# Two graph-attention layers in one kernel: the adjacency cast to bf16 in DRAM and turned by a transposing DMA, layer 0's TensorE work in smaller pieces

## The chip, the cores and the metric

The kernel runs on one core of a Trainium2 chip. The metric is the device time of one launch in microseconds (us). The kernel before took 3321.95 us, the median of three runs (3321.3 to 3324.14).

## What is computed

Sixteen graphs of 1024 nodes with 256 features each pass through two attention layers. Both use the same adjacency, which holds 0 or 1. Cut to what matters:

```python
# layer 0, per graph; 4 heads of 64
h = x @ W                                         # per head
weight[i, j] = leaky_relu(e_src[i] + e_dst[j]) where adj[i, j], else -1e9
o = relu(softmax(weight) @ h + bias) + h
x = layernorm(x + layernorm_per_head(o) * ln_gamma + ln_beta)
# layer 1, per graph; 8 heads of 32
n = layernorm(x) * gamma1 + beta1
attn = softmax(where(adj > 0, n @ n.T / sqrt(32), -inf)) @ n
x = x + attn
x = layernorm(x + gelu(layernorm2(x) @ W1 + b1) @ W2 + b2)
```

The adjacency arrives as 32-bit integers with queries as rows. The kernel wants it as a mask of one byte with keys on the partitions, so every 1024 x 1024 adjacency has to be cast and turned.

## The kernel before

**Two streams.** `layer0()` (line 987) and `layer1()` (line 1005) are Python generators. Each runs over the sixteen graphs, and layer 0 works on graph b+1 while layer 1 works on graph b. The order of instructions on TensorE, VectorE, ScalarE and GpSimd is the order in which Python issues them: the loop at lines 1058 to 1076 takes one step of one stream or of the other. A stream yields after each step with a number (how far it has come) and with the things that its next step needs. `COURSE` (line 1043) says how far layer 0 is to be for each point of layer 1, and `SLACK` how far it may stray from that when the stream that is due would have to wait. Small chains of VectorE, ScalarE and GpSimd work (normalisations, residuals) wait in a list, and `advance()` (line 466) issues those whose inputs are due. Only SyncE's queue, which carries DMAs, is ordered by the framework.

**Layer 0.** `prepare` (line 504) takes two blocks of 128 rows at a time. It turns x on TensorE (`transpose_rows`), multiplies with `w0e` (W and two extra columns per head; tile `ph`, 264 wide, two chunks of 128 in the contracted dimension, line 546), and evicts. `turn_mask` (line 509) takes one block `ak` of 128 adjacency rows, turns its eight 128 x 128 pieces on TensorE as bf16 into one PSUM bank, and writes them as the mask with one `Square` on ScalarE, which also counts the neighbours. The block comes by a casting DMA on GpSimd's queue (`load_adj`, line 492); three blocks are in flight (`load_adj(i + 3)`, line 523). `attention0` (line 587) has 32 steps per graph. A step's weights are two VectorE operations of 128 x 512 (line 598), issued three steps ahead (`AHEAD`), and its products are 16 matmuls in 64-column tiles (line 612).

**Layer 1.** `attention1` (line 740) has 32 steps per graph. A step computes four logit tiles (line 766, four matmuls with 32 rows each, side by side in the array), four exponentials on ScalarE (line 772), two VectorE products with the mask (line 778), and, three steps later, the products with the values (line 780). `mlp` (line 893) follows, in units of 16 matmul records.

**PSUM.** Four banks `ps` take logits and the first half of the MLP; two `po` take layer 1's sums; two `acc` (through `bank0`, line 390) take all of layer 0's: x turned, mask turned, `ph`, products, and a few transposes of layer 1 during its attention. A matmul with fp32 operands is two records in the trace, a bf16 transpose one.

Of the kernel before, what the change touches and what calls it, by code (L numbers as in the profile page):

```python
# [32 lines left out]
BF16 = mybir.dt.bfloat16  # L33
# [6 lines left out]
P = 128  # L40
# [143 lines left out]
def fast_path(  # L184
# [24 lines left out]
    nc = Pace(tc.nc)  # L209
    B, N, D = x.shape  # L210
    H0, _, HO = w0.shape
# [29 lines left out]
    memory = ctx.enter_context(tc.tile_pool(name="memory", bufs=2, space=bass.MemoryType.DRAM))  # L241
# [247 lines left out]
    adj_blocks = {}  # L489
    x_blocks = {}  # L490

    def load_adj(i):
        b, k = divmod(i, NB)
        if b < B:
            ak = adj_blocks[i] = three.tile([P, N], BF16, name="ak")
            nc.gpsimd.dma_start(ak, adj[b, k * P : (k + 1) * P, :])

    def load_blocks(i):
        b, k = divmod(i, NB // GB)
# [4 lines left out]
    def prepare(b, hb, esr, cbs, v0, dinv, mask):  # L504

        def turn_mask(k):
            i = b * NB + k  # L510
            ak = adj_blocks.pop(i)
            pt, _ = bank0([P, NB, P], BF16)
            for j in range(NB):
                nc.tensor.transpose(pt[:, j, :], ak[:, j * P : (j + 1) * P], identb)
            nc.scalar.activation(
                mask[k // BPH][:, :, k % BPH * P : (k % BPH + 1) * P],
                pt,
                AF.Square,
                bias=shift_c,
                scale=-(NEAR0 + NEAR1),  # L520
                accum_out=types[:, i : i + 1],
            )
            load_adj(i + 3)

        turning, scaling = [], []
        for k in range(0, NB, GB):
            i = b * (NB // GB) + k // GB
            load_blocks(i + 1)
            xk = x_blocks.pop(i)
            xT = one.tile([P, DC, GB * P], F32, name="xT")  # L530
            transpose_rows(xT, xk)
            yield 0.45, bank0_ready
            turn_mask(k)
            yield 0.5, bank0_ready, xT
            if k % BPH == 0:

                finish_norms(b - 1, k // BPH)
                hb.append(one.tile([P, BPH, D], F32, name=f"hb{k // BPH}"))
            for g in range(GB):
                if g == 0:  # L540

                    for chain in turning:
                        complete(chain)
                ph, _ = bank0([P, D + 2 * H0])
                for c in range(DC):
                    nc.tensor.matmul(ph, xT[:, c, g * P : (g + 1) * P], w0e[:, c, :], start=c == 0, stop=c == DC - 1)
                nc.scalar.copy(apart[g][:, :, 0], ph[:, D + H0 : D + 2 * H0])
                nc.scalar.activation(v0[:, k + g, :, HO], ph[:, D : D + H0], AF.Exp)
                nc.scalar.activation(dinv[:, k + g, :], ph[:, D : D + H0], AF.Exp, scale=-0.99)
                scaling.append(values0(v0[:, k + g, :, :], ph))  # L550
                begin(scaling[-1], "vector", ph)
                nc.scalar.copy(hb[-1][:, (k + g) % BPH, :], ph[:, 0:D])
                yield 0.9, bank0_ready
                if g == 0:
                    turn_mask(k + 1)
                    yield 0.5, bank0_ready, xT
# [30 lines left out]
    def attention0(b, hb, v0, esr, cbs, dinv, factors, mask, rinv):  # L587

        groups = [(n, pair) for n in range(NH) for pair in range(H0 // PAIR)]
        steps = [(n, hd, j) for n in range(NH) for hd in range(H0) for j in range(0, NB, PAIR)]

        def weights(n, hd, j):
            cb = cbs[n, hd // PAIR]
            p = four.tile([P, PAIR, HALF], F32, name="p0")
            for i in range(PAIR):
                nc.vector.scalar_tensor_tensor(
                    p[:, i, :],
                    cb[:, hd % PAIR, :],  # L600
                    dinv[:, j + i, hd : hd + 1],
                    mask[n][:, j + i, :],
                    op0=OP.max,
                    op1=OP.mult,
                )
            return p

        def products(p, hd, j, av):
            for i in range(PAIR):
                for q in range(BPH):  # L610
                    for at in range(0, P, TILE):
                        nc.tensor.matmul(
                            av[at : at + TILE, q, :],
                            p[:, i, q * P + at : q * P + at + TILE],
                            v0[:, j + i, hd, :],
                            start=j + i == 0 and q == 0,
                            stop=j + i == NB - 1 and q == BPH - 1,
                        )

        nc.vector.tensor_copy(factors, v0[:, :, :, HO])  # L620

        ps = [weights(*step) for step in steps[:AHEAD]]
        yield 1.0, bank0_ready, ps[0]
        for i, (n, hd, j) in enumerate(steps):
            if j == 0:
                av, bank = bank0([P, BPH, HO + 1])
                bank["busy"] = True
            products(ps.pop(0), hd, j, av)
            advance()
            if i + AHEAD < len(steps):  # L630
                ps.append(weights(*steps[i + AHEAD]))
            if j == NB - PAIR * AHEAD and hd % PAIR == PAIR - 1 and (n, hd // PAIR) in groups[:-2]:

                at = groups[groups.index((n, hd // PAIR)) + 2]
                cbs[at] = spread_factor(esr, *at)
            if j == NB - PAIR:
                h = hb[n][:, :, hd * HO : (hd + 1) * HO]
                residual = residual0(av, h, rinv[:, n * BPH : (n + 1) * BPH, hd])
                residuals[b, n, hd] = residual
                bank["busy"] = False  # L640
                bank["readers"] = [residual]
                begin(residual, "vector", av)
                if hd % PAIR == PAIR - 1:
                    norms[b, n, hd] = after0(b, n, hd, hb[n])
                    begin(norms[b, n, hd], "vector", done(residual), hb[n])
            yield (1.0, *ps[:1], *([bank0_ready] if j == NB - PAIR else []))

    def residual0(av, h, rinv):

# [384 lines left out]

    WORK0 = NB // GB * 3.25 + 2.0 + NB * H0 * 1.0
    REST1 = 3.5 * GB
    ATTN1 = REST1 + 2.0 + 2.5 * (NH * NB * H1 // QUAD)
    WORK1 = ATTN1 + NB // GB * (1.75 * FC / 2 + 3.5 * GB) - REST1  # L1040
    SLACK = 0.083
    STAY = 0.017
    COURSE = [(0.0, 1.0), (REST1, 1.0), (ATTN1, 1.32), (WORK1 - 12.0, 2.0), (WORK1, 2.0)]

    def wanted():
        b, done = place[1]
# [477 lines left out]
```

## Time and profile before

| | us |
|---|---|
| median of three runs | 3321.95 |
| the profiled execution, own time | 3326.4 |
| its span, first to last instruction | 3324.5 |
| TensorE busy (weight loads apart) | 3227.9 |
| VectorE busy | 2887.0 |
| ScalarE busy | 1944.0 |
| GpSimd busy | 546.5 |

In the trace one graph's layer 1 begins about every 201 to 207 us; the graph used below begins at 717.9 us and the next one at 919.3. From 717.9 to 843.0 lies its attention (with what is left of the MLP of the graph before at the front), from 843.0 to 919.3 its MLP. Layer 0's `prepare` for the next graph goes from 719.6 to 799.4. The first 110 us hold layer 0 of graph 0 alone, and after 3145 layer 1 of the last graph runs alone.

How to read it: busy time of TensorE is that of pipelined matmuls whose ends are modelled, so "busy" can hide a wait. More is learnt from the starts of consecutive groups in the timeline: from the start of one group to the start of the next is what it cost the engine. All helper-recorded operations stand under line 61; they are told apart by their tiles, such as `acc<-identb,ak` for the mask turned, `acc<-w0e,xT` for the product with W, `acc<-v,p` for layer 0's products, `ps<-nT` for layer 1's logits, `po<-p,v`, `po<-p,unit` and `po<-v,p` for layer 1's products, `ps<-yT,w_sb` and `po<-w_sb,hid` for the MLP.

### The profile page before, as it was taken

How to read it: one execution, taken by the hardware profiler on the slowest of the kernel's cores; microseconds unless marked ns; L12 is line 12 of the kernel's file. 1: busy time of each engine (PE TensorE's matmuls, PEld its weight loads, DVE VectorE, ACT ScalarE, POOL GpSimd, SP SyncE). 2: the span in 40 equal slices, each digit the busy share in tenths (PEclk: the TensorE clock that was granted, in tenths of full speed). 3: DMA queues.
4: the chain of work that ended last, by engine and by line, in shares of the span. 5: the costliest groups of instructions: out<-in, count | busy, mean ns of one | idle time of the engine just before them, and what ended most of it. 6: DMA issues, size and time to landing. Idle time of an engine off the chain costs nothing.

```text
span 3324.5 us, 148763 instructions
## 1 busy us (share of the span) xinstructions
PE 3227.9 (97%) x68257; PEld 2050.2 (62%) x68257; DVE 2887.0 (87%) x4943; ACT 1944.0 (58%) x4192; POOL 546.5 (16%) x552
## 2 busy tenths in 40 slices
PE   6899999999999999999999999999999999999988
PEld 4557575665756657566575755757566575665745
DVE  6898897988979889898988979889798898989983
ACT  2564747557375673846647366473755738466473
POOL 1202011020211202112020111202102021120300
PEclk9899999999999999999999999999999999999999
DMA  5201102021120211202112020110202112020000
GB/s 140 53 22 46 42 25 66 14 52 35 31 61 18 52 30 34 60 20 62 23 44 44 25 60 19 50 38 28 63 19 47 35 34 60 19 59 10 24 6 15
DMA packets 94732, 131.79 MB, mean 40 GB/s; under 512 B 9360, under 2 KB 60560, under 8 KB 94096
## 3 DMA queue, kind: packets, MB, share of 16 engines
q1 hardware_dynamic: 74080, 87.58, 8.4%
q0 software_dynamic: 18432, 33.56, 6.6%
q8 instruction: 536, 8.78, 1.1%
q10 hardware_dynamic: 1584, 1.05, 0.1%
q14 instruction: 100, 0.82, 0.1%
HBM read 138.68 MB, written 17.04 MB: 47 GB/s over the span
## 4 chain that ended last, share of the span: by engine, by line
PE 86%; DVE 10%; issue 2%; ACT 1%; DMA 0%; POOL 0%; ACTq 0%; SPq 0%; POOLq 0%; DVEq 0%
PE po L61 34%; PE ps L61 30%; PE acc L61 22%; DVE p L61 8%; DVE o L61 0%; ACT p L61 0%; DVE hb L61 0%; DVE st L61 0%; DVE z L61 0%; ACT oT L61 0%; DMA w0e<-in_L_gnn_W_dram 0%; ACT mask L61 0%; POOL r L61 0%; DVE x L61 0%; DMA v<-in_L_gnn_a_src_dram 0%
## 5 line engine op out<-in xcount | busy, mean ns | idle before, releaser
L61 ACT ACTIVATE p<-ps 128x512 f32<-128x512 f32 x2006 | 1041.0, 611 | 314.7 <-PE ps L61 304.6
L61 DVE TENSOR_TENSOR p<-p,mask 128x1024 f32<-128x1024 f32 x1024 | 1188.7, 1217 | 15.6 <-ACT p L61 15.6
L61 DVE SCALAR_TENSOR_TENSOR p<-cb,dinv,mask 128x512 f32<-128x512 f32 x1024 | 709.5, 743 | 4.1 <-PE acc L61 4.1
L61 PE MATMUL ps<-nT 32*128 32x512 f32 x4012 | 671.9, 643 | 0.0
L61 ACT ACTIVATE hid<-ps,b_sb 128x256 f32<-128x256 f32 x512 | 240.7, 473 | 677.3 <-PE ps L61 677.3
L61 PEld LDWEIGHTS po<-v,p 128*32 128x32 f32 x32768 | 391.5, 109 | 331.0 <-issue 284.6
L61 PE MATMUL acc<-v,p 128*64 128x65 f32 x16384 | 551.8, 225 | 15.8 <-DVE p L61 13.6
L61 PEld LDWEIGHTS acc<-v,p 128*64 128x64 f32 x16384 | 531.4, 139 | 56.9 <-DVE p L61 13.4
L61 PE MATMUL po<-p,v 128*32 128x512 f32 x2048 | 544.3, 606 | 0.0
L61 PE MATMUL po<-p,unit 128*32 128x512 f32 x2048 | 543.6, 606 | 0.0
L61 PE MATMUL po<-w_sb,hid 128*64 128x256 f32 x4096 | 479.5, 381 | 0.0
L61 PE MATMUL ps<-yT,w_sb 128*64 128x256 f32 x4096 | 470.6, 380 | 0.0
L61 PE MATMUL po<-v,p 128*32 128x33 f32 x32768 | 387.8, 198 | 15.7 <-issue 12.0
L61 PEld LDWEIGHTS ps<-yT,w_sb 128*64 128x64 f32 x4096 | 286.3, 137 | 139.7 <-issue 5.3
L61 PEld LDWEIGHTS po<-w_sb,hid 128*64 128x64 f32 x4096 | 279.9, 137 | 133.1 <-issue 3.9
L61 POOL TENSOR_SCALAR r<-mv 128x4 f32<-128x4 f32 (+1 forms) x128 | 87.9, 687 | 1289.2 <-DVE mv L61 1249.1
L61 POOL TENSOR_TENSOR r<-r,mhalf 128x8 f32<-128x8 f32 (+2 forms) x192 | 288.9, 1505 | 16.0
L61 PEld LDWEIGHTS ps<-nT 32*128 32x128 f32 x4012 | 218.0, 184 | 108.1 <-issue 45.0
L61 PEld LDWEIGHTS po<-p,v 128*32 128x32 f32 x2048 | 78.1, 108 | 324.8 <-issue 172.9
L61 DVE TENSOR_TENSOR z<-acc,bias_r 128x256 f32<-128x256 f32 x128 | 54.2, 423 | 209.4 <-ACT hb L61 209.1
L61 POOL DMA_DIRECT2D ak<-in_adj_dram x128 | 71.5, 559 | 961.5 <-PE acc L61 948.9
L61 PE MATMUL acc<-w0e,xT 128*128 128x264 f32 x512 | 151.0, 418 | 9.8 <-issue 6.5
(111 smaller groups left out, 2660.2 us busy)
## 6 DMA issues: line engine op xcount, KB each, us to landing
ak<-in_adj_dram POOLq DMA_DIRECT2D x128, 256.0 KB, 3.9
cb<-esr SPq DMA_DIRECT2D x64, 512.0 KB
xk<-in_x_dram SPq DMA_DIRECT2D x64, 256.0 KB
xl<-in_x_dram SPq DMA_DIRECT2D x32, 512.0 KB
out_dram<-zz SPq DMA_DIRECT2D x64, 256.0 KB
w_sb<-in_L_gnn_W_dram SPq DMA_DIRECT2D x2, 1024.0 KB
esr<-rows SPq DMA_DIRECT2D x64, 4.0 KB
v<-in_L_gnn_a_src_dram SPq DMA_DIRECT2D x2, 320.0 KB
```

The lines of the kernel that those rows point to most:

```text
L61: return method(*args, **kwargs)
```

## The change

For graphs 1 to 15 the adjacency no longer passes through TensorE. `cast_adj(b + 1)`, at the start of `prepare(b)`, issues two DMAs on GpSimd's queue that cast the two halves (512 rows each) of the next graph's adjacency from DRAM to bf16 in DRAM. `load_adj` then fills a block `ak` with two transposing DMAs on SyncE's queue, each 512 rows x 128 columns, and `turn_mask` is the `Square` alone, reading `ak` in SBUF. Graph 0 keeps the old way.

The product with W is cut in two: after the first of the two contracted chunks the stream yields, and `turn_mask` is called there. Its PSUM bank is held over the yield. Layer 0's products are cut in two likewise, one of the two key blocks each, with `advance()` between. The first three weights of a graph are issued with a yield after each. The course is set anew.

```diff
+    def cast_adj(b):
+        if b < B:
+            for n in range(NH):
+                casts[b, n] = memory.tile([HALF, N], BF16, name=f"adjb{n}")
+                nc.gpsimd.dma_start(casts[b, n], adj[b, n * HALF : (n + 1) * HALF, :])
...
             ak = adj_blocks[i] = three.tile([P, N], BF16, name="ak")
-            nc.gpsimd.dma_start(ak, adj[b, k * P : (k + 1) * P, :])
+            if b == 0:
+                nc.gpsimd.dma_start(ak, adj[b, k * P : (k + 1) * P, :])
+                return
+            n, first = divmod(k * PAIR, NB)
+            for e in range(PAIR):
+                nc.sync.dma_start(
+                    ak[:, e * HALF : (e + 1) * HALF],
+                    casts[b, n][:, (first + e) * P : (first + e + 1) * P],
+                    transpose=True,
+                )
...
         def turn_mask(k):
             i = b * NB + k
-            ak = adj_blocks.pop(i)
-            pt, _ = bank0([P, NB, P], BF16)
-            for j in range(NB):
-                nc.tensor.transpose(pt[:, j, :], ak[:, j * P : (j + 1) * P], identb)
+            pt = adj_blocks.pop(i)
+            if b == 0:
...
+            else:
+                n, first = divmod(k * PAIR, NB)
+                dst = mask[n][:, first : first + PAIR, :]
+                pt = pt.rearrange("p (e q) -> p e q", q=HALF)
...
+        cast_adj(b + 1)
...
-            yield 0.45, bank0_ready
-            turn_mask(k)
-            yield 0.5, bank0_ready, xT
+            yield 0.45, bank0_ready, xT
+            if b == 0:
+                turn_mask(k)
+                yield 0.0, bank0_ready, xT
...
-                ph, _ = bank0([P, D + 2 * H0])
+                ph, bank = bank0([P, D + 2 * H0])
+                bank["busy"] = True
                 for c in range(DC):
                     nc.tensor.matmul(ph, xT[:, c, g * P : (g + 1) * P], w0e[:, c, :], start=c == 0, stop=c == DC - 1)
+                    if c == 0:
+                        if b:
+                            turn_mask(k + g)
+                        yield (0.45,)
+                bank["busy"] = False
...
-        ps = [weights(*step) for step in steps[:AHEAD]]
-        yield 1.0, bank0_ready, ps[0]
+        ps = []
+        for step in steps[:AHEAD]:
+            ps.append(weights(*step))
+            yield 0.33, bank0_ready, ps[0]
...
-            products(ps.pop(0), hd, j, av)
+            p = ps.pop(0)
+            products(p, 0, hd, j, av)
+            advance()
+            yield (0.5,)
+            products(p, 1, hd, j, av)
             advance()
...
-            yield (1.0, *ps[:1], *([bank0_ready] if j == NB - PAIR else []))
+            yield (0.5, *ps[:1], *([bank0_ready] if j == NB - PAIR else []))
...
-    WORK0 = NB // GB * 3.25 + 2.0 + NB * H0 * 1.0
+    WORK0 = NB // GB * 2.25 + 2.0 + NB * H0 * 1.0
...
+    SLACK1 = 0.02
-    COURSE = [(0.0, 1.0), (REST1, 1.0), (ATTN1, 1.32), (WORK1 - 12.0, 2.0), (WORK1, 2.0)]
+    COURSE = [(0.0, 1.0), (REST1 + 3.0, 1.0), (ATTN1, 1.31), (WORK1 - 12.0, 2.0), (WORK1, 2.0)]
...
-            allowed = at0 < min(target + SLACK, place[1][0] + 2.05) if other == 0 else at0 > target - SLACK
+            slack = SLACK if place[1][1] >= ATTN1 else SLACK1
+            allowed = at0 < min(target + slack, place[1][0] + 2.05) if other == 0 else at0 > target - slack
```

More of the change, by code (lines that the diff above doesn't have):

```diff
@@ L490, in fast_path @@
     x_blocks = {}
+    casts = {}
+    def cast_adj(b):
[3 more added lines that the diff above has]
+                nc.gpsimd.dma_start(casts[b, n], adj[b, n * HALF : (n + 1) * HALF, :])
     def load_adj(i):
@@ L510, in turn_mask @@
             i = b * NB + k
-            ak = adj_blocks.pop(i)
-            pt, _ = bank0([P, NB, P], BF16)
-            for j in range(NB):
-                nc.tensor.transpose(pt[:, j, :], ak[:, j * P : (j + 1) * P], identb)
+            pt = adj_blocks.pop(i)
+            if b == 0:
+                ak = pt
+                pt, _ = bank0([P, NB, P], BF16)
+                for j in range(NB):
+                    nc.tensor.transpose(pt[:, j, :], ak[:, j * P : (j + 1) * P], identb)
+                dst = mask[k // BPH][:, :, k % BPH * P : (k % BPH + 1) * P]
+            else:
+                n, first = divmod(k * PAIR, NB)
+                dst = mask[n][:, first : first + PAIR, :]
+                pt = pt.rearrange("p (e q) -> p e q", q=HALF)
             nc.scalar.activation(
-                mask[k // BPH][:, :, k % BPH * P : (k % BPH + 1) * P],
+                dst,
                 pt,
@@ L552, in prepare @@
                 nc.scalar.copy(hb[-1][:, (k + g) % BPH, :], ph[:, 0:D])
-                yield 0.9, bank0_ready
-                if g == 0:
+                yield 0.45, bank0_ready
+                if g == 0 and b == 0:
                     turn_mask(k + 1)
-                    yield 0.5, bank0_ready, xT
+                    yield 0.0, bank0_ready, xT
             turning.append(turn_sources(esr, k, cbs))
@@ L606, in weights, with products @@
             return p
[L608 to L618, printed above, removed]
+        def products(p, i, hd, j, av):
+            for q in range(BPH):
+                for at in range(0, P, TILE):
+                    nc.tensor.matmul(
+                        av[at : at + TILE, q, :],
+                        p[:, i, q * P + at : q * P + at + TILE],
+                        v0[:, j + i, hd, :],
+                        start=j + i == 0 and q == 0,
+                        stop=j + i == NB - 1 and q == BPH - 1,
+                    )
         nc.vector.tensor_copy(factors, v0[:, :, :, HO])
-        ps = [weights(*step) for step in steps[:AHEAD]]
-        yield 1.0, bank0_ready, ps[0]
+        ps = []
+        for step in steps[:AHEAD]:
+            ps.append(weights(*step))
+            yield 0.33, bank0_ready, ps[0]
         for i, (n, hd, j) in enumerate(steps):
```

## The prediction

> **What bounds the kernel now.** I read the page's busy times and chain first.
>
> ```profile
> PE 3227.9 (97%) x68257; PEld 2050.2 (62%) x68257; DVE 2887.0 (87%) x4943; ACT 1944.0 (58%) x4192; POOL 546.5 (16%) x552
> PE 86%; DVE 10%; issue 2%; ACT 1%; DMA 0%; POOL 0%; ACTq 0%; SPq 0%; POOLq 0%; DVEq 0%
> ```
>
> TensorE carries 86% of the chain, VectorE 10%, no DMA counts. Then busy time by stage, for the graph that begins at 717.9: prepare with attention, the rest of attention, the MLP.
>
> ```profile
> 717.90:799.40 81.50, 80.80 (x1668) 42.87 (x1670) 66.54 (x106) 66.75 (x154) 12.02 (x15) 1.00 0.27 61
> 799.40:843.00 43.60, 43.26 (x1294) 25.35 (x1286) 43.31 (x55) 27.25 (x53) 0.00 (x0) 1.00 0.03 6
> 843.00:919.30 76.30, 76.30 (x1310) 59.23 (x1308) 69.91 (x150) 27.36 (x56) 22.09 (x20) 1.00 0.13 35
> ```
>
> Third column TensorE, fifth VectorE, sixth ScalarE. VectorE is full from 799 to 843 (43.31 of 43.60), at 82% before, at 92% in the MLP. TensorE looks full everywhere, so last I read the timeline, where starts tell waits.
>
> ```profile
> 738.88 0.62 PE L61 MATMUL po<-p,v 128*32 128x512 f32 x1
> ...
> 739.76 0.74 PE L61 MATMUL po<-v,p 128*32 128x33 f32 x64
> 740.44 0.62 PE L61 MATMUL acc<-identb,ak 128*128 128x128 bf16 x8
> 740.99 2.25 PE L61 MATMUL ps<-nT 32*128 32x512 f32 x8
> 743.17 0.62 PE L61 MATMUL po<-p,v 128*32 128x512 f32 x1
> ...
> 744.05 0.75 PE L61 MATMUL po<-v,p 128*32 128x33 f32 x64
> 744.73 1.16 PE L61 MATMUL acc<-w0e,xT 128*128 128x264 f32 x4
> 745.81 1.14 PE L61 MATMUL ps<-nT 32*128 32x512 f32 x8
> 746.88 0.62 PE L61 MATMUL po<-p,v 128*32 128x512 f32 x1
> ...
> 748.44 1.77 PE L61 MATMUL ps<-nT 32*128 32x512 f32 x8
> 750.14 0.62 PE L61 MATMUL po<-p,v 128*32 128x512 f32 x1
> ```
>
> Start to start, one attention step is logits 1.07 (745.81 to 746.88), products 0.88 and 0.68: 2.63. Between two steps lies "filler" of layer 0: the product with W costs 1.08 (744.73 to 745.81), the turned mask 0.55 (740.44 to 740.99). At 748.44 there was no filler and the logits took 1.70 (to 750.14): a hidden wait of 0.63. Four `ps` banks serve four logit tiles, and these come free only when ScalarE has done the exponentials:
>
> ```profile
> 746.97 2.06 ACT L61 ACTIVATE p<-ps 128x512 f32<-128x512 f32 x4 [0.42 <-PE ps L61]
> 749.60 2.07 ACT L61 ACTIVATE p<-ps 128x512 f32<-128x512 f32 x4 [0.56 <-PE ps L61]
> ```
>
> Logits 1.07 plus exponentials (2.1, and about 0.1 around them) make a floor of 3.25 per step. So a filler of 0.6 is free, an empty step wastes it, and a filler of 1.08 costs 0.46.
>
> [...] at 741.90 a mask `Square` (1.17, then 0.26 for its accumulator) stands ahead of the exponentials, and the logits at 740.99 take 2.18. [...]
>
> **The change, step by step.** Durations are of the profiled execution: own time 3326.4, span 3324.5, 0.13% above the median of 3321.95.
>
> *Turned masks leave TensorE.* 960 of 1024 transposes go: 120 groups at about 0.54, 65 us of work. But by the built order some five of eight groups per graph were alone between two attention steps, under the floor; there removal alone would give 0.07. What counts is what fills the steps now.
>
> *Pieces.* I took the instruction order of both built kernels for one graph and summed, over its 32 attention steps, 2.63 (1.07 where no products stand yet) plus filler, from starts in the trace; half a W product is 0.54, half a step of layer-0 products 0.47 and 0.15 for the change of array shape (the whole block at 807.51 takes 1.08). Before: 117.4 plain, and 121.9 with every step raised to 3.25, since six steps are empty while ten hold 1.08. Measured: 125.1 (717.9 to 843.0), so 3.2 more is lost to late ScalarE and VectorE. After: twelve steps hold half a W product, five half a product of layer 0, one is empty; 111.1 plain, 113.2 with the floor. To this come the other waits. They were 3.2; now more steps stand at the floor, and a `Square` with its accumulator (1.3) no longer fits under logits of 1.07: some 0.25 on seven of them, 1.7, partly paid before. I take 4.7. VectorE: 109.9 in this stage before (66.54 and 43.31), with 18 weights of 0.74 all at its end; the order leaves about 13, so some 106 in 118, just short of full at the end. Stage after: 117.9, a gain of 7.2. Ends: 115.2 (waits of 2) to 121.
>
> *Work handed to the MLP.* By the order, 912 records of layer-0 products lie there instead of 832: 80 x 0.029 = 2.3, and 0.3 for changes of shape: +2.6. My sum for that stage before gives 76.5 against 76.3 measured, without waits. VectorE there gets 2.5 steps x 1.4 = 3.5 more: 73.4 of 78.9, not yet full.
>
> Per graph 7.2 - 2.6 = 4.6; fifteen graphs: 69 us.
>
> *Casts.* 128 loads used 6.6% of sixteen engines' span, 1.7 each; one graph's cast moves the bytes of eight: 13.7 of all engines, with DRAM as target unmeasured. Between graphs it hides (DMA share 0.27 at most in the stages above), a whole graph ahead of its use. GpSimd issues 2 instead of 8; whoever queues behind there are the rstd chains, and they wait for VectorE. At the start it does not hide: the first 45 us have a DMA share of 0.96, and the first product with W starts at 19 behind loads of W and the attention vectors. The cast of graph 1 is queued right behind the first three blocks, also ahead of graph 0's other five. Bounds 0 and 20 us; I take 12, once.
>
> *Transposing DMAs.* 240, on SyncE. The trace has none. [...] Two serve a mask turn, which comes about every 10 us, three ahead: hidden, cost 0. On SyncE each waits for ScalarE's `Square`; behind it stand loads of x, stores of `esr` and the spread `cb`, used tens of us later. Without that cover, see the rival.
>
> *`Square` from SBUF.* ScalarE evicts 512 columns in 0.60 from PSUM and 0.63 from SBUF (`oT`): 120 x 0.03 = 3.6 at most, beside other work; I take 2.
>
> *Weights one by one* spread a burst of six VectorE operations (4.5); within the waits above.
>
> Sum: -69 + 12 + 2 = -55: 3321.95 - 55 = **3267**.
>
> **Rivals.** (a) *The banks still decide.* TensorE's saving turns into waits for `ps`: late `Square`s and VectorE (106 in a stage now shorter) hold attention at 121; then 4.1 - 2.6 = 1.5 per graph, 22 in all, less 12: 3312. For it: transposes under the floor were free. Against: halves fill the empty steps. (b) *More:* waits fall to 2 and the casts cost nothing: 7.3 x 15 = 110: 3212. Against: VectorE at 92% in the MLP. (c) *Slower: transposing DMAs are too slow,* one place and one price: masks arrive late and TensorE's written order waits. With t per DMA, five loads per graph beyond the three ahead wait 2t - 10 each; it outweighs the 3.7 per graph that are left from about t = 5.4. At 6: +150, 3417. [...] That the change isn't made is excluded by the order.
>
> **How the numbers follow.** Likeliest 0.60 (own range 3240 to 3295), (a) 0.19, (b) 0.08, (c) and any other slower way 0.13. Under 0.2% (6.6 us) a measurement of this kernel can't tell from none. Of (a) 0.14 is faster and 0.05 the same; so faster 0.82, same 0.05, slower 0.13. The range takes in (a) and most of (b): 3220 to 3318.
>
> **What would show it.** In the profile after: no `acc<-identb` beyond graph 0; W products in groups of two between attention steps; few empty steps and logit groups near 1.07 to 1.15; VectorE below 95% at the end of attention; MLP stage near 79; graphs about 197 apart; the first product with W some 12 later[...]. Wrong if attention stays above 121, if ScalarE's `Square` waits for the DMA of `ak`, or if VectorE fills the MLP.

## The result, and the profile after

The kernel after takes 3326.73 us (median of 18 runs, 3322.51 to 3332.32), the kernel before, beside it, 3322.75 (18 runs, 3318.3 to 3326.11). The ratio is 1.0013, 95% interval 1.0006 to 1.002: 0.1% slower, where 3267 was forecast, and outside the forecast range of 3220 to 3318.

From the page of the kernel after, TensorE's, VectorE's and ScalarE's busy time and the chain by engine:

```profile
PE 3184.2 (96%) x67297; PEld 1981.5 (60%) x67297; DVE 2885.1 (87%) x4943; ACT 1942.9 (58%) x4192; POOL 504.3 (15%) x462
PE 76%; DVE 16%; ACT 5%; issue 2%; POOL 1%; DMA 1%; POOLq 0%; ACTq 0%; DVEq 0%
```

TensorE has 44 us less to do, and its share of the chain falls from 86% to 76%; VectorE and ScalarE take over what it gave up. Busy time by stage of the kernel after, for the graph that begins at 732.1 (prepare with attention, the rest of attention, the MLP; columns as before):

```profile
732.10:817.60 85.50, 83.21 (x1760) 41.22 (x1758) 69.34 (x110) 72.07 (x161) 9.02 (x8) 0.98 0.28 58
817.60:854.20 36.60, 35.54 (x1060) 19.32 (x1058) 34.73 (x41) 22.88 (x47) 0.00 (x0) 1.00 0.05 11
854.20:933.50 79.30, 79.05 (x1399) 62.03 (x1387) 75.54 (x157) 26.34 (x55) 22.23 (x21) 1.00 0.23 59
```

The attention stage takes 122.1 (before 125.1) and the MLP 79.3 (before 76.3). Beside each other, from the starts in the two traces:

| us | before | after | difference |
|---|---|---|---|
| layer 1 of graph 0 begins | 110.2 | 120.2 | +10.0 |
| first graph, start to start | 205.0 | 210.1 | +5.1 |
| the next 14 graphs, mean of one | 202.16 | 201.16 | -1.00, so -14 |
| their attention stage, median | 125.3 | 122.05 | -3.25 |
| their MLP, median | 76.3 | 79.2 | +2.9 |
| from the last start to the end | 179.1 | 177.8 | -1.3 |

So the gain is 1.0 per graph, where 4.6 was forecast, and the start and the first graph eat it. Some 0.7 of the 1.0 is owed to two long graphs of the kernel before (205.2 and 207.1, the others about 201.5); by the medians of the two stages the gain is 0.35. The traced execution of the kernel before, at 3326.4, took longer than any of the 18.

Where the attention stage loses its time is seen in TensorE's timeline of the kernel after (start, us, operation; the last bracket is idle time and who ended it). The stretch is steps 10 to 12 of the same graph:

```profile
772.34 1.16 PE L61 MATMUL acc<-w0e,xT 128*128 128x264 f32 x4
773.43 1.14 PE L61 MATMUL ps<-nT 32*128 32x512 f32 x8
774.50 0.66 PE L61 MATMUL acc<-ident,oT 128*128 128x128 f32 x4
...
776.64 0.66 PE L61 MATMUL acc<-ident,xk 128*128 128x128 f32 x4
778.88 0.41 PE L61 MATMUL acc<-ident,apart 128*128 128x128 f32 x2 [1.58 <-DVE o L61]
779.22 1.38 PE L61 MATMUL ps<-nT 32*128 32x512 f32 x8
780.53 1.06 PE L61 MATMUL po<-p,v 128*32 128x512 f32 x1
...
783.97 1.14 PE L61 MATMUL ps<-nT 32*128 32x512 f32 x8
```

Both halves of a W product stand together in front of this step (772.34, four records). The step itself turns on TensorE a head's output (`oT`), new rows of x (`xk`) and `apart` (some of the extra columns of the product with W): three tiles for the two `acc` banks. `xk` takes the bank of the W product, and `apart` needs the one that `oT` holds until VectorE has read it. VectorE's queue in the kernel after at that time:

```profile
775.00 0.43 DVE L61 TENSOR_TENSOR z<-acc,bias_r 128x256 f32<-128x256 f32 x1 [0.88 <-ACT hb L61]
...
775.81 2.35 DVE L61 TENSOR_TENSOR p<-p,mask 128x1024 f32<-128x1024 f32 x2
778.08 0.20 DVE L61 RECIPROCAL ranges<-acc 128x8 f32<-128x8 f32 x1
778.31 0.42 DVE L61 TENSOR_TENSOR o<-acc,ranges 128x256 f32<-128x256 f32 x1
```

The two operations that free the bank (778.08, 778.31) could start when `oT` was written, at about 775.1. They stand behind the W product's `z`, which waited 0.88 for ScalarE, and behind two mask products. TensorE idles 1.58. This wait is in each of the 14 graphs, 1.54 to 1.59 long. In five of them, this one among them, it costs more than itself: the same products that took 0.62 now take 1.06. A view of the granted clock (fourth figure) says why:

```profile
779.22:780.53 1.31, 1.31 (x9) 0.80 0.58 199
780.53:782.24 1.71, 1.71 (x12) 0.50 0.01 2
782.24:783.28 1.04, 1.04 (x69) 0.50 0.76 252
```

TensorE's clock fell to half after the gap. Step 11 took 5.79 for 4.03 of listed work, step 12 took 4.75 for 3.27. The first loss is in all 14 graphs (5.79 or 5.80). The second is the clock's alone: step 12 takes 4.74 to 4.93 in the five graphs with the half clock and 3.27 in the nine without.

### The profile page after: what moved, and what is told of

It is laid out like the page before. It is cut to its first block, busy times and chain, and to the rows that moved or that the text cites. A ratio compares the mean times of both kernels' runs of the same rounds, so it can differ in the third digit from the quotient of the medians.

```text
span 3324.4 us, 147073 instructions
## 1 busy us (share of the span) xinstructions
PE 3184.2 (96%) x67297; PEld 1981.5 (60%) x67297; DVE 2885.1 (87%) x4943; ACT 1942.9 (58%) x4192; POOL 504.3 (15%) x462
## 4 chain that ended last, share of the span: by engine, by line
PE 76%; DVE 16%; ACT 5%; issue 2%; POOL 1%; DMA 1%; POOLq 0%; ACTq 0%; DVEq 0%
PE po L61 30%; PE ps L61 27%; PE acc L61 19%; DVE p L61 10%; ACT p L61 2%; POOL r L61 1%; DVE x L61 1%; DVE v L61 1%; ACT o L61 1%; DVE z L61 1%; ACT mask L61 1%; DMA w0e<-in_L_gnn_W_dram 1%; ACT hb L61 0%; DVE st L61 0%; DVE o L61 0%
## 5 line engine op out<-in xcount | busy, mean ns | idle before, releaser
L61 PE MATMUL ps<-nT 32*128 32x512 f32 x4012 | 654.5, 644 | 1.0 <-ACT p L61 1.0
L61 PE MATMUL acc<-v,p 128*64 128x65 f32 x16384 | 562.0, 225 | 19.5 <-DVE p L61 15.7
L61 PEld LDWEIGHTS acc<-v,p 128*64 128x64 f32 x16384 | 538.5, 139 | 64.6 <-DVE p L61 18.5
L61 PE MATMUL ps<-yT,w_sb 128*64 128x256 f32 x4096 | 480.6, 380 | 0.5 <-issue 0.5
L61 POOL TENSOR_SCALAR r<-mv 128x4 f32<-128x4 f32 (+1 forms) x128 | 79.0, 617 | 2259.6 <-DVE mv L61 2205.7
L61 PEld LDWEIGHTS ps<-yT,w_sb 128*64 128x64 f32 x4096 | 295.5, 137 | 124.4 <-issue 4.1
L61 POOL TENSOR_TENSOR r<-r,mhalf 128x8 f32<-128x8 f32 (+2 forms) x192 | 321.4, 1674 | 16.0
L61 PEld LDWEIGHTS ps<-nT 32*128 32x128 f32 x4012 | 204.5, 183 | 139.5 <-ACT p L61 79.3
L61 PE MATMUL acc<-w0e,xT 128*128 128x264 f32 x512 | 176.2, 433 | 30.4 <-ACT xT L61 18.1
L61 DVE TENSOR_TENSOR zz<-po,x 128x256 f32<-128x256 f32 x128 | 53.7, 420 | 103.9 <-PE po L61 103.9
## 6 DMA issues: line engine op xcount, KB each, us to landing
adjb<-in_adj_dram POOLq DMA_DIRECT2D x30, 1024.0 KB, 12.7
```

The costliest lines, as they stand in the source:

```text
L61: return method(*args, **kwargs)
```

## The experiments

Eighteen kernels ran. All times in the table are medians beside runs of the kernel before on the same chip (3322.8 to 3328.4); start, first graph, and the medians of attention and MLP are read from starts in each trace.

| kernel | us | ratio to before, 95% | start | first graph | attention | MLP |
|---|---|---|---|---|---|---|
| late_cast | 3329.21 | 1.0014 to 1.0028 | 120.7 | 212.1 | 121.55 | 79.2 |
| plain_load | 3322.46 | 0.999 to 1.0007 | 113.2 | 211.7 | 122.2 | 79.2 |
| pieces_only | 3305.46 | 0.9939 to 0.9973 | 113.1 | 203.1 | 119.4 | 80.8 |
| w_whole | 3352.78 | 1.0076 to 1.011 | 118.9 | 207.0 | 124.1 | 79.25 |
| half_masked_after | 3271.37 | 0.9827 to 0.986 | 121.8 | 203.9 | 117.9 | 79.25 |
| half_masked_before | 3346.08 | 1.0058 to 1.0098 | 110.3 | 204.5 | 124.35 | 78.9 |
| mask_by_dma | 3309.21 | 0.9941 to 0.9974 | 112.4 | 207.4 | 123.35 | 76.7 |
| course_late | 3286.86 | 0.9878 to 0.9911 | 120.1 | 207.3 | 117.4 | 80.8 |
| course_start | 3312.49 | 0.9956 to 0.9981 | 118.5 | 208.0 | 121.05 | 79.2 |
| course_end | 3283.7 | 0.9858 to 0.9891 | 119.7 | 207.1 | 116.85 | 80.8 |
| turn_two_late | 3284.01 | 0.9869 to 0.9902 | 112.2 | 212.4 | 117.4 | 80.8 |
| pieces_late | 3322.26 | 0.9988 to 1.0006 | 112.8 | 205.8 | 121.0 | 80.5 |
| shift_two | 3299.27 | 0.9892 to 0.9925 | 120.1 | 207.8 | 119.8 | 79.3 |
| before_end | 3396.44 | 1.0177 to 1.0211 | 110.0 | 207.7 | 126.05 | 81.2 |
| pieces_127 | 3338.24 | 1.0016 to 1.0038 | 116.3 | 206.6 | 117.6 | 84.8 |
| dma_only | 3359.8 | 1.0072 to 1.0106 | 126.7 | 206.5 | 124.6 | 78.45 |
| end_123 | 3297.4 | 0.9901 to 0.9934 | 120.5 | 207.7 | 117.4 | 81.2 |
| turn_two_end | 3277.33 | 0.9843 to 0.9876 | 111.3 | 209.8 | 116.7 | 80.8 |

### Which part of the change lost the time

The first theory (A) was that the casts cost their time at the start and that waits of the attention stage took the rest; the rivals were the pieces (B) and the transposing DMAs (C). Four kernels.

**late_cast.** The cast of graph 1 moves behind graph 0's first blocks.

```diff
-        cast_adj(b + 1)
+        if b:
+            cast_adj(b + 1)
         for k in range(0, NB, GB):
+            if b == 0 and k == GB:
+                cast_adj(1)
```

> The changed kernel with the cast of graph 1 issued at graph 0's second pair of blocks instead of its first. Layer 1 of graph 0 began 10.0 us later with the change (120.2 instead of 110.2). Theory A (at the start the cast shares the DMA engines with the loads of W; everything else is the attention stage): the first product with W is back near 19 us, layer 1 of graph 0 begins near 110, the time is 3316 to 3318, the interval of graphs stays at 201. Theory C (the DMAs hold the later graphs too): graph intervals fall as well. If the start is longer for another reason (SyncE's transposing DMAs ahead of the spread factors): layer 1 still begins near 118 and the time stays at 3326.

The first W product came back from 28.5 to 19.9, but layer 1 still began at 120.7: something in the second half of graph 0's preparation took the time again. Theory A had the place where the casts collide; moving them was no cure.

**plain_load.** No casts and no transposing DMAs; the mask of graphs 1 to 15 comes from the untouched load, so it is not turned. TensorE's order is that of the kernel after.

```diff
-            if b == 0:
+            if True:
                 nc.gpsimd.dma_start(ak, adj[b, k * P : (k + 1) * P, :])
                 return
...
-        cast_adj(b + 1)
```

> The changed kernel with neither cast nor transposing DMA: each block of adjacency comes by the old casting DMA and is used as if it were already turned (the mask is not turned, so attention is masked wrongly; all instructions of TensorE, VectorE and ScalarE stay). Theory A (waits of the attention stage on ScalarE and VectorE took the gain): only the start comes back, 3314 to 3318, interval 201, attention about 122. Theory C (transposing DMAs or casts delay the masks, x or the factors): interval 197, about 3260.

3322.46: all the DMAs of the change together cost 4 us. The start is 7 us earlier, the first graph 1.6 longer, and the attention stage is not shorter (122.2). Theory C falls.

**pieces_only.** Everything of the change, but the masks of all graphs are turned on TensorE.

```diff
-            if b == 0:
+            if True:
                 turn_mask(k)
-                yield 0.0, bank0_ready, xT
+                yield 0.5, bank0_ready, xT
...
-    WORK0 = NB // GB * 2.25 + 2.0 + NB * H0 * 1.0
+    WORK0 = NB // GB * 3.25 + 2.0 + NB * H0 * 1.0
```

> All of the change's pieces and its course, but every graph's mask turned on TensorE as before, with the old yields for it: no casts, no transposing DMAs. Plain sum of TensorE per graph by starts of the trace before: attention 115.8 with the floor, MLP 80.9. Theory A (removed transposes are worth little because the stage waits anyway): attention 122 to 124, interval 203 to 205, about 3350 to 3380 with the start as before. Theory B (the removal is worth its 4 us per graph and the pieces lose as much, by their two changes of array shape and the bank held): interval about 205 to 206, 3390.

Both sides missed: at 3305.46 it beats both kernels. **w_whole** leaves the change as it is, but W's product in one piece with the `Square` ahead of it.

```diff
+                if b:
+                    turn_mask(k + g)
                 ph, bank = bank0([P, D + 2 * H0])
...
-                    if c == 0:
-                        if b:
-                            turn_mask(k + g)
-                        yield (0.45,)
...
-                yield 0.45, bank0_ready
+                yield 0.9, bank0_ready
```

> The changed kernel with the product with W in one piece again (the mask's Square is issued ahead of it); layer 0's products stay in two. Half a product costs 0.643 instead of the 0.54 I took. Theory A: the floor rises from 113.2 to 116.5 since more attention steps stand without filler, waits stay: attention 122 to 125, interval 201 to 204, 3326 to 3370. Theory B (pieces ate the gain: 14 shape changes and the bank held over the yield): attention below 120, interval below 199, under 3295.

26 us slower than the kernel after, so theory B falls. As a price for one piece the 26 can't be read: the edit gave a new order too, in which TensorE idles 2.11 to 2.12 at step 27 of each of the 14 graphs for a `po` bank that VectorE reads late, some 30 us in all. That the pieces are a gain rests on pieces_only, 17 us below the kernel before, though with another course. From pieces_only to the kernel after, which turns its masks by DMA and has the order that comes of it, 21 us are lost, although work is taken away: 7 at the start, 7 in the first graph, 10 in the 14 graphs after it, less 2 at the end.

### VectorE, ScalarE or the course

Two theories were left for an attention stage of 122 with 113 of listed work: VectorE is full (D), or ScalarE's list is late (E). Four kernels.

**half_masked_after** and **half_masked_before**, one edit in each of the two kernels:

```diff
-            for p in ps:
+            for p in ps[:1]:
```

> The changed kernel, with the mask multiplied onto only the first of the two score tiles of each layer-1 step: half of layer 1's mask products are left out, so VectorE has about 1.2 us less to do in each of 32 steps of an attention stage; TensorE's list of instructions is unchanged (111 us of plain work in the attention stage, 113 with the steps that run into the exponentials). Theory D, VectorE: the 9 us of other waits in the changed kernel's attention stage are VectorE's, which is full from its middle on; they fall to about 3, the stage from 122 to about 116, the time by 15 x 6 = 90 us to about 3235. Theory E, ScalarE and the order of its list (Square, turned parts and score exponentials one behind another): VectorE's load matters little, the stage stays at 120 or more, time 3290 to 3320.

> The kernel before, with the mask multiplied onto only the first of the two score tiles of each layer-1 step (half of layer 1's mask products are left out). It has the transposes on TensorE, 117 us of plain work in the attention stage, 122 with the steps that run into the exponentials, and only 3 us of other waits. Theories D and E both say that little can be had here: attention 122 to 124 instead of 125, time 3275 to 3310. If it falls by as much as the changed kernel does with the same edit, VectorE was a limit before the change as well, and cannot be why the removal of the transposes brought nothing.

3271.37 and 3346.08, and neither can be read as a test of load. The order of work is planned from a price for every instruction, VectorE's too, so leaving work out re-orders TensorE's list, against what I had written: in the first kernel `xk` moved from step 11 to step 12, away from `oT`. In the second, half of VectorE's mask products gone made the kernel *slower*: in 13 of its 14 graphs TensorE idles 1.99 to 2.61 for an `oT` that ScalarE writes late. That was the first hint that the order weighs more than an engine's load.

**mask_by_dma**, without casts, block loads and `Square` from graph 1 on:

```diff
-                pt = pt.rearrange("p (e q) -> p e q", q=HALF)
+                nc.gpsimd.dma_start(
+                    mask[n][:, first : first + PAIR, :],
+                    adj[b, k * P : (k + 1) * P, :].rearrange("p (e q) -> p e q", q=HALF),
+                )
+                load_adj(i + 3)
+                return
```

> The changed kernel without the Square that makes masks from the adjacency: from graph 1 on the mask bytes are written by a converting DMA straight from the adjacency, not turned, and the sums that the Square collected are left at zero; no casts, no transposing DMAs. So the masks are wrong in orientation and the check of the adjacency's kinds is left out. It takes some 1.2 us x 8 of ScalarE's time per graph away, and with it the Squares that stand ahead of exponentials, and TensorE's transposes as in the changed kernel. Theory E (ScalarE's list holds the attention stage): the stage falls from 122 to 117 or less, time 3235 to 3260. Theory D (VectorE): the stage stays within 1 us of 121, and only the start is better, as with the untransposed load: 3305 to 3322.

3309.21, with an attention stage of 123.35 and 2.5 us less in the MLP, so 1.2 less for both: far from what E asked for. Its list changed as well (layer-0 products went from the MLP to the stage), so this speaks against E but is no measure of a `Square`.

**course_late** changes two numbers:

```diff
-    COURSE = [(0.0, 1.0), (REST1 + 3.0, 1.0), (ATTN1, 1.31), (WORK1 - 12.0, 2.0), (WORK1, 2.0)]
+    COURSE = [(0.0, 1.0), (REST1 + 14.0, 1.0), (ATTN1, 1.25), (WORK1 - 12.0, 2.0), (WORK1, 2.0)]
```

> The changed kernel with another course: layer 0's next graph may begin some 10 us later in the attention stage and gets 1.25 instead of 1.31 of its plan by the end of it, so that the first W product stands about 20 us in and 4 steps' halves of layer-0 products move from the attention stage to the MLP, exactly as many as there are in the kernel with the pieces alone (3305 us). Nothing is left out. Theory D (VectorE is asked for too much too early because the room that the transposes took was filled with layer-0 work): attention falls from 122 to about 119 while the MLP grows from 79.3 to 80.8, so 3305 to 3315. Theory E (without the transposes as filler the steps run into ScalarE whatever the course): 113.2 + 9 = 122 in the attention stage and 80.8 in the MLP, 15 x 1.5 = 22 us more, about 3345.

3286.86, below what either theory had said: two numbers of the course bring 40 us. The next four kernels take them apart: **course_start** has 14.0 with 1.31, **course_end** 3.0 with 1.25, **turn_two_late** is course_late with graph 1's masks turned on TensorE too (`b <= 1` in place of `b == 0`, casts from graph 2 on), **pieces_late** is pieces_only with 14.0 and 1.28.

> The changed kernel with the first half of the later course alone: layer 0's next graph begins some 10 us later in the attention stage, but the end of the stage still asks for 1.31 of its plan. The MLP keeps its list (79.1 us). Theory D2 (what costs is that layer 0's work begins too early, so that scalings, residuals and Squares crowd the engines at the stage's start): most of the 40 us that the later course won comes with this edit, 3285 to 3300. Theory D1 (what costs is the amount of VectorE work inside the attention stage): the W products are now crowded into the later part where VectorE is full, so nothing or a loss, 3320 to 3345.

> The changed kernel with the second half of the later course alone: layer 0's work may begin as early as in the change, but the stage's end asks for 1.25 of its plan instead of 1.31, so that four half steps of layer-0 products move to the MLP (80.9 us instead of 79.1), and with them four half steps of VectorE's weights. Theory D1 (the amount of VectorE work inside the attention stage): 3287 to 3297, most of the 40 us. Theory D2 (the early start): attention stays near 121 and the MLP grows, 3325 to 3350.

> The changed kernel with the later course, and with the masks of graph 1 turned on TensorE as those of graph 0 are; the casts and transposing DMAs begin with graph 2, so that none of them runs while graph 0 is prepared. Nothing is left out. If the late start (layer 1 at 120 instead of 110 to 113 us) and the long first graph (207 instead of 198 us) come from the casts, the transposing DMAs ahead of the spread factors in SyncE's queue and the Squares of graph 1: layer 1 starts near 113, the first interval is 200 to 203, the time 3270 to 3277. If they come from the pieces and from the preparation of the MLP's weights in the first graph: start 117 to 120 and first interval 205 or more, 3280 to 3288.

> The pieces alone (masks turned on TensorE, no casts, no transposing DMAs), with the later course: layer 0's next graph some 10 us later in the attention stage, and 1.28 instead of 1.31 of its plan by its end (its plan is four units longer). It asks whether the later course, and not the turning by DMA, is what the 3287 us are owed to. Plain work in its attention stage is then about 114, 117.4 with the steps that run into the exponentials, the MLP 79.3 to 81. Theory D (the course that fits depends on the filler that is left: with the transposes the old one was near its best): 3300 to 3325. Rival F (any kernel with pieces gains from the later course, and the turning by DMA is worth nothing): 3265 to 3290.

turn_two_late (3284.01) gets the early start back, 112.2, but its first graph takes 212.4, so graph 1's casts and transposing DMAs explain the late start and not the long first graph. pieces_late (3322.26) is 17 slower than pieces_only, so the later course is no gain to every kernel with pieces, and rival F falls.

course_end has all of the 40 us, course_start a third, which looked like the amount of VectorE work in the stage (theory D1). But a comparison of the starts of all 32 steps of one graph did not: in the graph shown above, course_end begins step 31 6.5 us sooner, and 5.3 of these lie before step 13, at steps 10 to 12 above all (in a graph without the half clock 3.8 lie there). And course_start shows the same wait in a new place; its waits of TensorE, over one attention stage (in us: total, times, longest):

```profile
PE acc L61 <- DVE o L61: 1.9, 1, 1.9
```

There three halves of W stand together ahead of step 19, which holds `oT`, `xk` and `apart`: the crowded step moved from 11 to 19 with the later start. So theory G: three tiles for two banks in one step, and the reader late in VectorE's queue.

### The crowded step, tried by itself

**shift_two** changes one number and no amount of work.

```diff
-    COURSE = [(0.0, 1.0), (REST1 + 3.0, 1.0), (ATTN1, 1.31), (WORK1 - 12.0, 2.0), (WORK1, 2.0)]
+    COURSE = [(0.0, 1.0), (REST1 + 5.0, 1.0), (ATTN1, 1.31), (WORK1 - 12.0, 2.0), (WORK1, 2.0)]
```

> The changed kernel with layer 0's start in the attention stage two units of the course later (REST1 + 5.0 in place of REST1 + 3.0), 1.31 as it was. The amount of work of every kind in the attention stage and in the MLP (79.1 us) is the same; what changes is that at steps 10 to 12 one half of W stands where two stood, and the turning of a head's output no longer shares its step with the turning of new rows of x. Theory G (that collision, for one of the two shared banks): the 4 to 5 us that were lost before step 13 are back in each graph, the stage 117.5, the time 15 x 4.5 = 67 lower than 3327, 3255 to 3280. Theory D1 (the amount of VectorE work in the stage): nothing, 3318 to 3330.

3299.27, 27 us below the kernel after; by the ratios to the kernel before it is 35, since the kernel before ran slower beside it (3328.43). G had asked for 47 to 72, D1 for at most 9. TensorE's timeline of shift_two at the same steps, and the line with which VectorE frees `oT`'s bank:

```profile
769.08 0.66 PE L61 MATMUL acc<-ident,oT 128*128 128x128 f32 x4
...
771.31 0.71 PE L61 MATMUL acc<-w0e,xT 128*128 128x264 f32 x2
771.96 1.14 PE L61 MATMUL ps<-nT 32*128 32x512 f32 x8
...
774.58 0.66 PE L61 MATMUL acc<-ident,xk 128*128 128x128 f32 x4
775.08 0.38 PE L61 MATMUL acc<-ident,apart 128*128 128x128 f32 x2
775.39 1.14 PE L61 MATMUL ps<-nT 32*128 32x512 f32 x8
```

```profile
771.57 0.42 DVE L61 TENSOR_TENSOR o<-acc,ranges 128x256 f32<-128x256 f32 x1
```

`xk` and `apart` now stand a step after `oT`, and between `xk` and `apart` nothing waits. VectorE had read `oT`'s bank by 772.0, and the clock stays whole in all 14 graphs. In this graph step 13 begins at 48.3 instead of 51.9 after the stage's start. That is more than the usual gain: the graph of the kernel after that is compared here is one of the five with the half clock, and only in such a graph are 4 to 5 us near. In the nine others step 13 begins at 50.4, so the edit brings 2.1 there. The median of the stage falls by 2.25.

**end_123** asks whether less work in the stage goes on paying (1.23 in place of 1.25).

> The changed kernel with 1.23 in place of 1.31 of layer 0's plan by the end of the attention stage; five half steps of layer-0 products move to the MLP (81.4 us), against four with 1.25 (80.9). Its list has no place where two halves of W stand ahead of a step with both kinds of turning. Sum of the attention stage with the steps that run into the exponentials 112.7 (with 1.25: 112.4). Theory G with the sums: 0.8 us more per graph than with 1.25, 3290 to 3300. Theory D1 (each half step of VectorE's weights that leaves the stage brings some 10 us): 3265 to 3278.

3297.4, worse than course_end by 14, inside what G said. D1 falls. What is left between shift_two and course_end is 12 us by the ratios. By the medians of 14 graphs the stage is 3.0 shorter, among other things by 0.8 at step 5, 0.9 at steps 10 to 12 and 0.75 at step 27, with 1.5 more in the MLP; no run tried these by themselves.

**before_end** (the kernel before, 1.26 for 1.32), **pieces_127** (pieces_only, 1.27 for 1.31) and **dma_only** (the turning by DMA with W, products and first weights whole) say what belongs to which part.

> The kernel before with 1.26 instead of 1.32 of layer 0's plan asked for by the end of the attention stage: 8 half steps of layer-0 products (4 whole ones) move to the MLP, whose list grows from 76.3 to 80.9 us, while the plain work of the attention stage falls from 117.4 to 112.5, from 121.9 to 118.9 with the steps that run into the exponentials. The floor keeps 1.9 of the 4.9, so both sums say slower by 1.6 us per graph, 3340 to 3352. Theory D1 would have VectorE's relief take it down, 3285 to 3310, as in the changed kernel.

> The pieces alone (masks turned on TensorE) with 1.27 in place of 1.31: three half steps of layer-0 products move to the MLP, 82.3 instead of 80.9 us; the attention stage's sum with the steps that run into the exponentials falls from 115.8 to 113.5. Its list has no step with two W halves next to a crowded one. By the sums 0.9 us less per graph, 3290 to 3300. If it gets to 3284 or lower, the turning by DMA is worth nothing beside a better course; above 3300, the pieces had their best course already.

> The turning by DMA alone: W's products, layer 0's products and the weights whole as before, the changed kernel's course. Its attention stage has 111.0 of plain work, but 117.9 with the steps that run into the exponentials, since whole pieces leave more steps empty; MLP 78.6. With some 5 us of other waits 201.5 per graph plus the later start: about 3330. If the collisions cost it more, as in the kernel with W whole (3353): 3345 to 3375. A time below 3310 would mean that the pieces are what costs, which nothing so far says.

before_end misses all sums: 3396.44. It too has a step at which TensorE waits in every graph, but not for a bank: at step 11 it idles 2.02 for `oT` itself, which ScalarE writes late. In 8 of the 14 graphs a half clock follows. 4.9 us of work left the stage, and the stage grew by 0.75. In pieces_127 (3338.24, above all that the sums said) the MLP got the work and could not take it; its busy time in an MLP stage of 84.9 (VectorE is the third engine):

```profile
844.50:929.40 84.90, 84.21 (x1500) 64.89 (x1499) 82.67 (x170) 28.58 (x58) 20.87 (x19) 1.00 0.10 30
```

VectorE 82.67 of 84.9, where the list says 82.3 for TensorE. dma_only is slow (3359.8), so the turning by DMA alone, on this course, is a loss of about 30 us. But its order has, like w_whole's, a wait of 2.18 to 2.27 for a `po` bank in each of the 14 graphs, which comes to as much.

**The best version, turn_two_end:** course_end, with graph 1's masks turned on TensorE as in turn_two_late.

> The changed kernel with 1.25, and the masks of graph 1 turned on TensorE as those of graph 0, casts and transposing DMAs from graph 2 on. With the other later course the same edit gave the start 8 us back, and the first graph's interval took 5 of them. If that interval's growth is the order of that course: 3268 to 3276. If the first graph waits for the preparation of layer 0's second half and of the MLP's weights in any order: 3278 to 3284, the same as with 1.25 alone.

3277.33, ratio 0.9859 (0.9843 to 0.9876), between the two ranges. Layer 1 begins at 111.3, the first graph takes 209.8 instead of 207.1, so 8.4 come back and 2.7 go. The stages are those of course_end (attention 116.7, MLP 80.8), and that is near what the prediction had meant: busy time of course_end, attention and MLP of one graph,

```profile
721.50:837.90 116.40, 115.51 (x2754) 58.24 (x2752) 102.60 (x146) 95.09 (x207) 9.56 (x8) 1.00 0.19 46
837.90:918.70 80.80, 80.80 (x1458) 63.43 (x1449) 76.94 (x162) 26.68 (x55) 22.01 (x20) 1.00 0.22 58
```

with VectorE and ScalarE as busy as in the kernel after (102.60 against 104.07 in the attention stage) and 5.7 us less time.

## Why the prediction was wrong

**The step that failed is the term "other waits", taken at 4.7.** The sum of listed work with the floor was 113.2; the stage took 122.05, so the waits were 8.85, which is 4.15 too many in each graph. I had taken 3.2, as before, and 1.5 for a `Square` that does not fit under the logits. The runs showed in its place one crowded step: 1.6 of idle in each graph on a shared bank, and after it, in 5 of 14, a half clock that costs another 1.5. Taken away by itself (shift_two) it gives 27 to 35 us, and the stage falls to 119.8. So it is about half of what the term missed. The waits that are left, 119.8 - 113.2 = 6.6, are still 1.9 above my 4.7, and what they are stays open. With a course that has no such step and less work in the stage (course_end) they are 116.85 - 112.4 = 4.4, close to the 4.7. The list was in front of me: the order that I summed had two halves of W ahead of a step with `oT`, `xk` and `apart`. I priced each entry and did not ask which bank it needs and where that bank's reader stands.

The term isn't the whole miss. The two traces differ by -0.2 us where -55 was forecast: the 14 graphs miss 3.6 each, 50 in all, and the first graph misses 9.7 (+5.1 where -4.6 was forecast); the start, the `Square` and the end give 5 back.

**Turned masks leave TensorE: right in kind.** 44 us less TensorE time was no gain by itself. pieces_only against course_end, with the same products in the MLP, sizes it: 3305.46 to 3283.7, 22 us, after 11 more at the start and in the first graph. This compares the best course found for each, of three tried with the masks turned on TensorE and of six with the DMAs. On the course that the change came with, it was a loss of 21, 14 of them at the start and in the first graph. One transpose takes 221 ns in the trace before and eight overlap to 0.55.

**Pieces: right in kind, one price off.** Halves fill the empty steps, and pieces_only gains 17; what W in one piece costs by itself is not shown. Half a W product costs 0.64 start to start, not 0.54, which under the floor adds 0.02 to a step (2.63 + 0.64 = 3.27).

**The MLP: right.** +2.9 for +2.6; 79.2 for 79.

**The casts: right in place, priced too high.** Layer 1 begins 10.0 later, against 12; but plain_load, without the DMAs, takes 7.0 back, and pieces_only, which has none either, begins at 113.1, so some 3 come with the pieces. **Not priced: the first graph, +5.1.** In its first steps TensorE waits for the normalised rows `sq` that it turns into `nT`; from the waits of the kernel after, 119 to 150:

```profile
PE acc L61 <- ACT sq L61: 7.8, 1, 7.8
```

The kernel before waits 4.3 at that place and pieces_only 3.6; plain_load, without these DMAs, 7.0. So it isn't the DMAs. What makes it late stays open.

**Transposing DMAs: right that they cost nothing in the stages** (without them, in plain_load, the attention stage is 122.2). Their issue takes 1.25 us of SyncE's queue each (median of 240; 1.12 to 2.43); no `Square` waited for them (ScalarE's idle time before the 120 of them is 0.0), and rival (c) is excluded. Their landing the trace doesn't show; that they would be hidden was my estimate, without a measured time for one. **`Square` from SBUF:** 1.169 against 1.115, 0.054 x 120 = 6.5 on ScalarE, beside other work; my 2 is neither shown nor denied.

**The rivals.** (a) was the nearest: attention at 121, 3312. It had the direction, banks, and VectorE's lateness; it named the `ps` banks, and the runs show `acc`. That it was given 0.19 is the same mistake as the 4.7: I had nothing from the trace that excluded it. Of the signs I named, "wrong if attention stays above 121" came true.

## What to carry to other kernels

A sum over an instruction list needs a second pass: for each tile in a small shared pool, find the operation that frees its buffer and count what stands ahead of it in that engine's queue; steps in which more tiles start than there are buffers are where the sum breaks. Where a planner sets the order, an edit of work is an edit of the order too, and a part of a change is judged only on a course that suits it: here one number moved the kernel after by 43 us, more than any part of the change; w_whole and dma_only, each run on one course alone, can't be read as prices. And an experiment that leaves work out tests load only if the order stays the same.

## What the runs showed of the hardware that was not expected

- **A granted clock of 0.5 followed some TensorE gaps of 1.45 to 2.45 us, and not others of like length.** A gap of 1.58 us was followed by it in 5 of 14 graphs (kernel after), one of 1.90 in 9 of 14 (course_start), one of 2.02 in 8 of 14 (before_end), those of 2.34 and 2.45 in both cases (before), one of 1.32 in none of 14 (end_123). Of three of 1.45 or 1.46, one was followed by it (course_end) and two not (before, shift_two). Length alone does not settle it: the last graph of the kernel after has three gaps of 2.61, and none was followed by a half clock. What else counts is not shown. In the kernel after, the graphs with the half clock took 202.0 on average, those without 200.7. In the kernel before, its two long graphs, 205.2 and 207.1 against 201.5, are the two with it, and with the gaps.
- **A stage can get longer when work leaves it.** before_end moved 4.9 us of work from the attention stage to the MLP; the MLP grew by 4.9, the attention stage by 0.75, and a graph took 4.7 more on average.
- **A cast from DRAM to DRAM** of half a graph (2 MB read, 1 MB written) landed in 12.7 us in the median.
